# Gated cross-attention: another order of loads, stores and weight sums in the setup, and a later attention transpose

## The chip, the cores and the metric

The kernel runs on one core of a Trainium2 chip, in float32 throughout. The metric is device time in microseconds (us) from the first to the last instruction, as the median of repeated runs. The kernel before takes 1005.09 us (three runs, 1005.05 to 1005.89).

## The reference, cut to what matters

```python
def reference(hidden_states, memory, W_mem, W_gate, b_gate, norm_w):   # 8x1024x1024, 8x64x512
    memory_proj    = einsum('bme,de->bmd', memory, W_mem)              # mp
    scores         = einsum('bnd,bmd->bnm', hidden_states, memory_proj) / sqrt(D)
    attn           = softmax(scores, axis=-1)
    memory_context = einsum('bnm,bmd->bnd', attn, memory_proj)
    gate_input     = concatenate([hidden_states, memory_context], axis=-1)
    gate           = sigmoid(einsum('bnf,df->bnd', gate_input, W_gate) + b_gate)
    fused          = hidden_states + gate * memory_context
    return fused * rsqrt(mean(fused ** 2) + 1e-06) * norm_w
```

The gate's product splits in two: x times the first half of W_gate (W1 below), and the memory context times the second half (W2). Since the context is attn times mp, the second part is attn times (mp times W2), and mp times W2 plus the bias is a small matrix (512 x 1024) that is made once.

## The kernel before

**Setup.** The memory (512 rows for the whole batch) is multiplied by W_mem into eight banks of PSUM (`pm`), and VectorE copies these to the four tiles `mpT`, two column chunks each. From there three things happen.

- `mpT` itself is stored to DRAM as `mpd` (lines 233 to 235). Each batch later loads its part, `mpb`, for the scores.
- `mpT` is transposed back to rows by VectorE, into one large tile `mpq`, and stored as `mgd[0]` (lines 236 to 249). `mpq` lies in the pool `xqpool`, which has one buffer, and that buffer is also the staging tile `xq` for x. So x can't be loaded before the stores of `mpq` have landed.
- TensorE makes mp times W2 in eight pieces of 128 x 512, n = 0 to 7 (`pg`, lines 430 to 435). VectorE adds the bias of each into a staging tile `g`, and the tile is stored as `mgd[1]` (lines 436 to 438). The staging tiles are two buffers in turn, `mg` and `attnT`, so piece n waits until the store of piece n-2 has landed.

VectorE also works on W1 between these pieces. The main product is done as Strassen-Winograd in two levels: seven outer products (o = 1 to 7), each of seven inner ones (A to F, A twice). The sums of W1's blocks that this needs are the list `w1_tasks` (lines 262 to 270): four outer sums of 128 x 2048 and 28 inner ones of 128 x 512. They are handed out behind the pieces n = 0 to 4 in equal parts. Behind piece 5 come six transposes of x (the first part of the list `first`, line 422) and GpSimd's first sums (`inner_s`), behind piece 6 the rest of `first`. x is loaded behind piece 0 (`load_xq(0)`, line 440), and the norm's weight too.

**The main loop.** x is worked in 16 quads of 512 rows. A quad is 49 slots; a slot is one inner product, two by two matmuls of 128 x 128 by 128 x 256. The outer products run in the order o = 1, 6, 7, 5, 4, 2, 3. Work of other engines is hung on slots by hand: `at(slot, fn)` puts it in the program ahead of that slot's matmuls, in the order in which it was hung, and `keep_in_program_order` holds each engine's instructions in program order. `plan(q)` (line 472) hangs a quad's own work; the end of an outer product hangs the norm's work into the next quad (lines 729 to 745). Around the change, counted from a quad's first slot:

- 7: scores (`psT` on TensorE, copied to `sT`), and two sums of x for the outer products; 9: the scores are transposed (`sc`); 10: softmax, first half (maximum and difference on VectorE, exponential on ScalarE); 13: second half (sum, reciprocal, and the product that makes `e` the attention).
- 17: `transpose_attn`: TensorE transposes `e` into `pa`, ScalarE copies it into `attnT` with four copies.
- 20: `attn_difference`: VectorE takes one difference within `attnT`.
- 17 and 18: `square`, ScalarE's sums of squares of the quad before; with the second goes a square root. 9 to 14, 23 and 29: `norm` on VectorE.
- 25: the first use of `attnT` on TensorE (`pc`).

All loads and stores but the residual's go through the queue of SyncE (`load`, line 95), which issues in program order.

Of the kernel before, what the change touches and what calls it, by code (L numbers as in the profile page):

```python
# [15 lines left out]
P = 128  # L16
# [4 lines left out]
def tile_gated_cross_attention_rmsnorm(  # L21
# [43 lines left out]
    QT = 4 * P  # L65
    QPB = N // QT
    NQ = B * QPB
    BM = B * M
    KD = D // P
    KE = E // P  # L70
    H = 512
    C = 256
    NPAIR = BM // P
    SCALE = 1.0 / float(D) ** 0.5
    Q4 = D // 4
# [3 lines left out]
    xqpool = ctx.enter_context(tc.tile_pool(name="xqpool", bufs=1))  # L79
    apool = ctx.enter_context(tc.tile_pool(name="apool", bufs=1))  # L80
    rot = ctx.enter_context(tc.tile_pool(name="rot", bufs=2))
    small = ctx.enter_context(tc.tile_pool(name="small", bufs=1))
# [6 lines left out]
    def mm(o, lhsT, rhs, start, stop):  # L89
        pin(nc.tensor.matmul(o, lhsT, rhs, start=start, stop=stop, skip_group_check=True))  # L90

    def tt(eng, o, a, b, op):
        pin(eng.tensor_tensor(o, a, b, op))  # L93

    def load(o, i):
        pin(nc.sync.dma_start(o, i))

    def t4k(pool, shape, tag, name):
        return pool.tile(shape, F32, tag=tag, name=name)
# [7 lines left out]
    def bank(n, shape, name):  # L107
        return ps.tile(shape, F32, tag=banks[n % 5], name=name)
# [36 lines left out]
    for h in range(2):  # L145
        for i in range(4):
            load(w1[h][32 * i : 32 * (i + 1), :, :], w1r[i][:, 4 * h : 4 * h + 4, :])
    R11, R21, R12, R22, T4, T1, T2 = range(7)
    outer_b = {
        o: w1[h][:, :, c * H : (c + 1) * H]  # L150
# [6 lines left out]
    def w_op(o, s):  # L157
        if s >= T4:
            return inner_t[o][:, s - T4, :, :]
        k, n = {R11: (0, 0), R21: (1, 0), R12: (0, 1), R22: (1, 1)}[s]  # L160
        return outer_b[o][:, 2 * k : 2 * k + 2, n * C : (n + 1) * C]

    nw_sb = const.tile([P, D], F32, name="nw_sb")
# [7 lines left out]
    mpd = dram.tile([P, KD, BM], F32, name="mpd")  # L171
    mgd = dram.tile([2, BM, D], F32, name="mgd")
# [14 lines left out]
    def order_wm(k):  # L187
# [18 lines left out]
    mpT = [  # L206
        t4k(rot, [P, 2, BM], tag, f"mpT_{tag}_{i}")
        for tag in ("l2", "u")
        for i in range(2)
    ]  # L210

    def mp_rows(j, q):
        return mpT[j // 2][:, j % 2, q * P : (q + 1) * P]


    mpq = t4k(xqpool, [P, 4 * 4, Q4], "xq", "mpq")
    pm = [bank(j, [P, BM], f"pm{j}") for j in range(5)]
    pm += [ps_ctx.tile([P, BM], F32, tag="ctx", name=f"pm{j}") for j in (5, 6)]
    pm += [ps.tile([P, BM], F32, tag="sc", name="pm7")]
# [10 lines left out]
                )  # L230
    for j in range(KD):
        pin(nc.vector.tensor_copy(mpT[j // 2][:, j % 2, :], pm[j]))
    for j in range(0, KD, 2):
        src = mpT[j // 2]
        load(mpd[:, j : j + 2, :], src)
        for g in range(2):
            pin(
                nc.vector.transpose(
                    mpq.rearrange("p s (j r) -> p s j r", r=32)[
                        :, 8 * g : 8 * g + 8, j : j + 2, :  # L240
                    ],
                    src[:, :, g * C : (g + 1) * C].rearrange("p j (s c) -> p s j c", c=32),
                )
            )
    for i in range(4):
        load(
            mgd[0, :, i * Q4 : (i + 1) * Q4].rearrange("(s c) e -> c s e", c=32),
            mpq[32 * i : 32 * (i + 1), :, :],
        )


    def outer_sum(o, a, b):
        tt(nc.vector, outer_b[o], outer_b[a], outer_b[b], ALU.subtract)

    def inner_sums(o):
        for s, a, b in ((T1, R12, R11), (T2, R22, T1), (R12, R22, R12), (T4, R21, T2)):
            yield lambda s=s, a=a, b=b: tt(
                nc.vector, w_op(o, s), w_op(o, a), w_op(o, b), ALU.subtract
            )
# [6 lines left out]
        lambda: outer_sum(7, 3, 7),  # L266
        *(f for o in (7, 5) for f in inner_sums(o)),
        lambda: outer_sum(4, 2, 6),
        *(f for o in (6, 4, 2, 3) for f in inner_sums(o)),
    ]  # L270


    xq, A, S, L2, O = {}, {}, {}, {}, {}
    sTs, attns, attnTs, scs, mps, mgs = {}, {}, {}, {}, {}, {}
    KH = KD // 2

    def where(q, t=0):
        return q // QPB, (q % QPB) * QT + t * P

    def load_xq(q):  # L280
        b, n0 = where(q)
        xq[q] = t4k(xqpool, [P, 16, Q4], "xq", f"xq{q}")
        src = x[b, n0 : n0 + QT, :].rearrange("(s c) (i e) -> i c s e", c=32, i=4)
        for i in range(4):
            load(xq[q][32 * i : 32 * (i + 1), :, :], src[i])

    def transpose_x(q, t, half):

# [44 lines left out]
    def inner_s(q, o, part):  # L333
        l11, l12, l21, l22 = quarters(left(q, o))
        if part == 0:
            L2[q, o] = t4k(rot, [P, 4, 2, P], "l2", f"l2_{q}_{o}")
        s1, s2, s3, s4 = (L2[q, o][:, i, :, :] for i in range(4))
        if part == 0:
            tt(nc.gpsimd, s1, l21, l22, ALU.add)
            tt(nc.gpsimd, s2, s1, l11, ALU.subtract)  # L340
        else:
            tt(nc.gpsimd, s3, l11, l21, ALU.subtract)
            tt(nc.gpsimd, s4, l12, s2, ALU.subtract)
# [85 lines left out]
    done, n = 0, 0  # L429
    for h in range(2):  # L430
        cols = slice(h * H, (h + 1) * H)
        for q in range(NPAIR):
            pg = bank(n, [P, H], f"pg2_{h}_{q}")
            for k in range(KD):
                mm(pg, mp_rows(k, q), w2[k][:, cols], k == 0, k == KD - 1)
            stage = t4k(small, [P, H], ("mg", "attnT")[n % 2], f"g2_{h}_{q}")
            tt(nc.vector, stage, pg, bias_sb[:, cols], ALU.add)
            load(mgd[1, q * P : (q + 1) * P, cols], stage)
            if n == 0:
                load_xq(0)  # L440
                load(nw_sb, norm_w.partition_broadcast(P))
            if n < 5:
                while done < len(w1_tasks) * (n + 1) // 5:
                    w1_tasks[done]()
                    done += 1
            elif n == 5:
                for f in first[:6]:
                    f()
                for part in range(2):
                    inner_s(0, 1, part)  # L450
            elif n == 6:
                for f in first[6:]:
                    f()
            n += 1
# [7 lines left out]
    def at(slot, fn, *args):  # L462
        due.setdefault(slot, []).append(lambda: fn(*args))

    def mid(key, fn, *args):
        beside.setdefault(key, []).append(lambda: fn(*args))
# [5 lines left out]
    def plan(q):  # L472
        t0 = SLOTS * q
        nxt = q + 1 < NQ
        order = [o for o, _ in ORDER]
        for i, o in enumerate(order):
            for part, t in ((0, 1), (1, 5)):
                if i + 1 < len(order):
                    at(t0 + 7 * i + t, inner_s, q, order[i + 1], part)
                elif nxt:  # L480
                    at(t0 + 7 * i + t, inner_s, q + 1, order[0], part)
        at(t0 + 7, scores, q)
        at(t0 + 7, outer_s, q, 3)
        at(t0 + 7, outer_s, q, 4)
        at(t0 + 9, transpose_scores, q)
        at(t0 + 10, softmax_a, q)
        at(t0 + 13, softmax_b, q)
        at(t0 + 17, transpose_attn, q)
        at(t0 + 20, attn_difference, q)
        if not nxt:  # L490
            at(t0 + 5, load_last)
            return
        at(t0 + 2, load_xq, q + 1)
        for t in (2, 3):
            mid((q, 5), transpose_x, q + 1, t, 0)
            mid((q, 2), transpose_x, q + 1, t, 1)
        for i, t, half in ((36, 0, 0), (38, 1, 0), (43, 0, 1), (45, 1, 1)):
            at(t0 + i, transpose_x, q + 1, t, half)
        mid((q, 3), outer_s, q + 1, 1)
        mid((q, 3), outer_s, q + 1, 2)  # L500
        if (q + 1) % QPB == 0:
            at(t0 + 10, load_mp, (q + 1) // QPB)
            at(t0 + 49, load_mg, (q + 1) // QPB)

    slot = 0

    def step():
# [241 lines left out]
    for q in range(NQ):  # L749
        plan(q)  # L750
        for o, ext in ORDER:
            outer_product(q, o, ext)
# [29 lines left out]
```

## Time and profile before

| engine | busy, us | share of the span |
|---|---|---|
| TensorE (PE) | 975.3 | 97% |
| its weight loads (PEld) | 766.3 | 76% |
| VectorE (DVE) | 766.4 | 76% |
| GpSimd (POOL) | 687.3 | 68% |
| ScalarE (ACT) | 317.6 | 32% |

How to read it: the span is 1005.2 us. A busy TensorE is one that has a matmul under way, so the waits to look for are the places where that record has a gap. In a timeline, a row gives the start, the duration, the engine, the line, the operation, what is written from what, the shapes and the number of merged instructions; in brackets stands how long the engine sat idle before the row, and what ended that. Line 93 and line 96 are helpers, so rows are told apart by their tiles. The trace numbers no tiles: `it` and `t` are W1's inner and outer sums, `a` transposed x, `l` GpSimd's sums of it, `u` VectorE's running sums.

### The profile page before, as it was taken

The page shows a single profiled execution, that of the slowest core. Times are in us where ns is not written, and L with a number is a line of the kernel's source. Part 1 is how long each engine was busy: PE and PEld are TensorE (multiplying, and loading weights), DVE is VectorE, ACT ScalarE, POOL GpSimd, SP SyncE. Part 2 cuts the span into 40 slices and gives each one's busy share as a digit, 9 for nine tenths or more (in the row PEclk, how much of TensorE's full clock was granted, in tenths as well). Part 3 has the DMA queues.
Part 4 walks back from the last instruction along what each step waited for, and adds up shares of the span by engine and source line. Part 5 has one row for each costly group of instructions (what it writes and reads, how often), then busy time and mean ns, then how long its engine had stood idle before and what let it go on. Part 6 is the DMA issues. An engine that isn't in the chain of part 4 may idle for free.

```text
span 1005.2 us, 14277 instructions
## 1 busy us (share of the span) xinstructions
PE 975.3 (97%) x4944; PEld 766.3 (76%) x4944; DVE 766.4 (76%) x1486; ACT 317.6 (32%) x588; POOL 687.3 (68%) x851
## 2 busy tenths in 40 slices
PE   6998999999999999999999999999999999999995
PEld 4443788878878887888788788878888887888783
DVE  2556567878878787878788787878787887878777
ACT  0000113424331514333242415233333424152344
POOL 0001477878878687878788786878687887868772
PEclk9999899999999999999999999999999999999998
DMA  9995609273643828182735647291926465381612
GB/s 206 231 258 126 131 1 179 84 137 116 128 113 92 181 66 176 63 173 100 144 94 112 144 103 160 60 192 63 178 85 123 112 134 126 84 189 53 178 64 84
DMA packets 72056, 126.76 MB, mean 126 GB/s; under 512 B 12848, under 2 KB 49712, under 8 KB 71984
## 3 DMA queue, kind: packets, MB, share of 16 engines
q1 hardware_dynamic: 63344, 94.39, 37.3%
q0 software_dynamic: 8640, 31.46, 16.7%
q8 instruction: 39, 0.64, 0.3%
q14 instruction: 33, 0.27, 0.1%
HBM read 85.98 MB, written 39.85 MB: 125 GB/s over the span
## 4 chain that ended last, share of the span: by engine, by line
PE 83%; DVE 13%; issue 1%; DMA 1%; SPq 1%; ACT 0%; POOL 0%; DVEq 0%; ACTq 0%
PE kA L90 17%; PE pc L90 11%; PE kE L90 9%; PE kD L90 8%; PE kF L90 8%; PE kB L90 8%; PE kC L90 7%; PE psT L90 6%; PE pg L90 5%; DVE gate L547 4%; DVE gate L93 3%; PE pm L90 2%; DVE e L93 2%; DVE u L93 1%; DMA wm<-in_w_mem_t 1%
## 5 line engine op out<-in xcount | busy, mean ns | idle before, releaser
L93 POOL TENSOR_TENSOR gate<-gate,u 128x256 f32<-128x256 f32 x336 | 269.0, 831 | 122.4 <-DVE u L93 102.3
L93 POOL TENSOR_TENSOR l<-a 128x256 f32<-128x256 f32 x128 | 125.4, 980 | 162.1 <-DVE a L296 95.1
L518 ACT ACTIVATE gate<-gate 128x512 f32<-128x512 f32 x128 | 79.0, 629 | 397.4 <-DVE gate L93 397.4
L90 PE MATMUL pc<-mg,attnT 64*128 64x256 f32 x512 | 127.4, 389 | 0.0
L90 PE MATMUL kB<-it,l 128*128 128x256 f32 x448 | 116.0, 382 | 2.5 <-POOL l L93 2.5
L547 DVE SCALAR_TENSOR_TENSOR gate<-gate,ss,nw_sb 128x512 f32<-128x512 f32 x120 | 116.3, 979 | 1.1
L90 PE MATMUL kD<-it,l 128*128 128x256 f32 x448 | 115.9, 381 | 0.0
L90 PEld LDWEIGHTS pc<-mg,attnT 64*128 64x128 f32 x512 | 90.6, 186 | 29.7 <-issue 21.2
L90 PE MATMUL kA<-w,a 128*128 128x256 f32 x384 | 99.6, 382 | 1.7 <-DVE a L296 1.4
L90 PEld LDWEIGHTS kB<-it,l 128*128 128x128 f32 x448 | 85.5, 191 | 14.5 <-POOL l L93 2.9
L90 PEld LDWEIGHTS kD<-it,l 128*128 128x128 f32 x448 | 84.5, 191 | 11.0
L93 DVE TENSOR_TENSOR gate<-gate,pc 128x512 f32<-128x512 f32 x128 | 87.1, 681 | 5.8 <-ACT gate L518 5.8
L296 DVE STREAM_TRANSPOSE a<-xq 128x512 f32<-128x512 f32 x128 | 86.0, 693 | 0.0
L90 PEld LDWEIGHTS kA<-w,a 128*128 128x128 f32 x384 | 73.4, 192 | 13.0 <-DVE a L296 2.2
L93 POOL TENSOR_TENSOR l<-s 128x256 f32<-128x256 f32 x96 | 77.7, 809 | 8.1 <-PE kF L90 5.6
L93 DVE TENSOR_TENSOR u<-u,kB 128x256 f32<-128x256 f32 x112 | 46.8, 418 | 43.7 <-PE kB L90 39.7
L662 ACT COPY u<-kA 128x256 f32<-128x256 f32 x112 | 40.4, 361 | 92.2 <-PE kA L90 92.1
L90 PE MATMUL kE<-it,a 128*128 128x256 f32 x256 | 69.3, 393 | 0.0
L90 PE MATMUL kC<-w,l 128*128 128x256 f32 x256 | 66.7, 384 | 2.2 <-DVE g L93 2.2
L90 PE MATMUL kA<-t,s 128*128 128x256 f32 x256 | 67.4, 386 | 0.0
L93 DVE TENSOR_TENSOR gate<-gate,kE 128x256 f32<-128x256 f32 x112 | 45.3, 417 | 27.5 <-PE kE L90 22.6
L90 PE MATMUL kF<-w,l 128*128 128x256 f32 x256 | 65.7, 379 | 0.0
(102 smaller groups left out, 1961.4 us busy)
## 6 DMA issues: line engine op xcount, KB each, us to landing
xq<-in_x SPq DMA_DIRECT2D x64, 512.0 KB, 9.6
gate<-in_x POOLq DMA_DIRECT2D x60, 512.0 KB, 8.3
out<-gate SPq DMA_DIRECT2D x60, 512.0 KB, 2.6
w<-in_w_gate_t SPq DMA_DIRECT2D x32, 128.0 KB, 4.5
w<-in_w_gate_t SPq DMA_DIRECT2D x8, 512.0 KB, 14.5
mg<-mgd SPq DMA_DIRECT2D x16, 256.0 KB, 4.1
mgd<-mpq SPq DMA_DIRECT2D x4, 512.0 KB, 11.7
mgd<-g SPq DMA_DIRECT2D x8, 256.0 KB, 2.1
```

What stands on the lines that cost most here:

```text
L90: pin(nc.tensor.matmul(o, lhsT, rhs, start=start, stop=stop, skip_group_check=True))
L93: pin(eng.tensor_tensor(o, a, b, op))
L296: nc.vector.transpose(A[key][:, :, r * P : (r + 1) * P].rearrange("p j (s c) -> p s j c", c=32), xq[q].rearrange("p s (j r) -> p s j r", r ...
L518: pin(nc.scalar.activation(g, g, AF.Sigmoid))
L547: nc.vector.scalar_tensor_tensor(g[:, cols], g[:, cols], rstd[:, t % 2 : t % 2 + 1], nw_sb[:, cols], ALU.mult, ALU.mult,)
L662: pin(nc.scalar.copy(p1, kb["A"]))
```

## The change

Five edits go together.

1. mp's rows get four staging tiles of 128 x 1024 in the pool of transposed x (`a11` to `a22`) instead of one tile in x's own buffer. The eight transposes of 128 x 512 become sixteen of 128 x 256, and the four stores of 512 KB sixteen of 128 KB.
2. With x's buffer free, `load_xq(0)` and the load of `norm_w` move ahead of all stores. Behind them come the sixteen stores of `mgd[0]`, then the four of `mpd`, then the eight of the gate's pieces.
3. The gate's pieces have three staging tiles in turn: `mg`, `attnT`, `mpb`.
4. Eight of the 32 sums of W1 (the inner sums of o = 2 and 3) leave the setup for slots 2 to 5 and 10 to 13 of the first quad.
5. In every quad `transpose_attn` moves from slot 17 to 18 and `attn_difference` from 20 to 21.

The aim is to have x in early, to let VectorE wait less for stores in the setup, and to make room for the sums in the first quad.

```diff
+    xq = {}
+
+    def load_xq(q):
+        b, n0 = q // QPB, (q % QPB) * QT
+        xq[q] = t4k(xqpool, [P, 16, Q4], "xq", f"xq{q}")
+        src = x[b, n0 : n0 + QT, :].rearrange("(s c) (i e) -> i c s e", c=32, i=4)
+        for i in range(4):
+            load(xq[q][32 * i : 32 * (i + 1), :, :], src[i])
...
-    mpq = t4k(xqpool, [P, 4 * 4, Q4], "xq", "mpq")
+    mpq = [t4k(apool, [P, 4, Q4], f"a{i}{j}", f"mpq{i}{j}") for i in (1, 2) for j in (1, 2)]
...
-    for j in range(0, KD, 2):
-        src = mpT[j // 2]
-        load(mpd[:, j : j + 2, :], src)
-        for g in range(2):
+    load_xq(0)
+    load(nw_sb, norm_w.partition_broadcast(P))
+    for g in range(4):
+        for j in range(0, KD, 2):
             pin(
                 nc.vector.transpose(
-                    mpq.rearrange("p s (j r) -> p s j r", r=32)[
-                        :, 8 * g : 8 * g + 8, j : j + 2, :
-                    ],
-                    src[:, :, g * C : (g + 1) * C].rearrange("p j (s c) -> p s j c", c=32),
+                    mpq[g].rearrange("p s (j r) -> p s j r", r=32)[:, :, j : j + 2, :],
+                    mpT[j // 2][:, :, g * P : (g + 1) * P].rearrange(
+                        "p j (s c) -> p s j c", c=32
+                    ),
                 )
             )
-    for i in range(4):
-        load(
-            mgd[0, :, i * Q4 : (i + 1) * Q4].rearrange("(s c) e -> c s e", c=32),
-            mpq[32 * i : 32 * (i + 1), :, :],
-        )
+        for i in range(4):
+            load(
+                mgd[0, g * P : (g + 1) * P, i * Q4 : (i + 1) * Q4].rearrange(
+                    "(s c) e -> c s e", c=32
+                ),
+                mpq[g][32 * i : 32 * (i + 1), :, :],
+            )
+    for j in range(0, KD, 2):
+        load(mpd[:, j : j + 2, :], mpT[j // 2])
...
-        *(f for o in (6, 4, 2, 3) for f in inner_sums(o)),
+        *(f for o in (6, 4) for f in inner_sums(o)),
     ]
-
-
-    xq, A, S, L2, O = {}, {}, {}, {}, {}
+    w1_last = [f for o in (2, 3) for f in inner_sums(o)]
...
-            stage = t4k(small, [P, H], ("mg", "attnT")[n % 2], f"g2_{h}_{q}")
+            stage = t4k(small, [P, H], ("mg", "attnT", "mpb")[n % 3], f"g2_{h}_{q}")
             tt(nc.vector, stage, pg, bias_sb[:, cols], ALU.add)
             load(mgd[1, q * P : (q + 1) * P, cols], stage)
-            if n == 0:
-                load_xq(0)
-                load(nw_sb, norm_w.partition_broadcast(P))
...
-        at(t0 + 17, transpose_attn, q)
-        at(t0 + 20, attn_difference, q)
+        at(t0 + 18, transpose_attn, q)
+        at(t0 + 21, attn_difference, q)
...
+    for i, fn in enumerate(w1_last):
+        at((2, 3, 4, 5, 10, 11, 12, 13)[i], fn)
```

More of the change, by code (lines that the diff above doesn't have):

```diff
@@ L268, in tile_gated_cross_attention_rmsnorm @@
         lambda: outer_sum(4, 2, 6),
-        *(f for o in (6, 4, 2, 3) for f in inner_sums(o)),
+        *(f for o in (6, 4) for f in inner_sums(o)),
     ]
-    xq, A, S, L2, O = {}, {}, {}, {}, {}
+    w1_last = [f for o in (2, 3) for f in inner_sums(o)]
+    A, S, L2, O = {}, {}, {}, {}
     sTs, attns, attnTs, scs, mps, mgs = {}, {}, {}, {}, {}, {}
@@ L278, in where @@
         return q // QPB, (q % QPB) * QT + t * P
[L280 to L285, printed above, removed]
     def transpose_x(q, t, half):
```

## The prediction

> **What bounds the kernel now.** I read the page first: shares of the span, then the chain that ended last.
>
> ```profile
> PE 975.3 (97%) x4944; PEld 766.3 (76%) x4944; DVE 766.4 (76%) x1486; ACT 317.6 (32%) x588; POOL 687.3 (68%) x851
> PE 83%; DVE 13%; issue 1%; DMA 1%; SPq 1%; ACT 0%; POOL 0%; DVEq 0%; ACTq 0%
> ```
>
> TensorE is the bound. An edit that removes no matmul can win only where TensorE has a gap, so I read its timeline for gaps. There are two kinds. The first is at the seam between setup and main loop (TensorE, 36 to 190 us):
>
> ```profile
> 90.81 3.60 PE L90 MATMUL pg<-w,mpT_u 128*128 128x512 f32 x8
> 95.78 1.13 PE L90 MATMUL kA<-w,a 128*128 128x256 f32 x4 [1.38 <-DVE a L296]
> 99.42 2.04 PE L90 MATMUL kB<-it,l 128*128 128x256 f32 x4 [2.50 <-POOL l L93]
> 103.63 2.05 PE L90 MATMUL kC<-w,l 128*128 128x256 f32 x4 [2.17 <-DVE g L93]
> 110.98 3.67 PE L90 MATMUL psT<-a,mpb 128*64 128x256 f32 x32
> ```
>
> From the end of `pg` (94.4) to `psT` (110.98) pass 16.6 us for seven inner products, which take 0.86 each in later quads, 6.1 in all. Some 10.5 us are open here: gaps, and products at half pace behind them. VectorE holds the end: kC uses the PSUM bank of the gate's last piece `g`, which VectorE empties late. Why late, its own timeline says:
>
> ```profile
> 57.10 2.29 DVE L93 TENSOR_TENSOR t<-w,t 128x2048 f32<-128x2048 f32 x1 [5.30 <-DMA w<-in_w_gate_t]
> 70.64 0.69 DVE L93 TENSOR_TENSOR g<-pg,bias_sb 128x512 f32<-128x512 f32 x1 [5.19 <-DMA mgd<-g]
> 85.15 0.69 DVE L93 TENSOR_TENSOR g<-pg,bias_sb 128x512 f32<-128x512 f32 x1 [7.88 <-DMA mgd<-g]
> 95.03 3.66 DVE L296 STREAM_TRANSPOSE a<-xq 128x512 f32<-128x512 f32 x6
> 102.83 0.65 DVE L93 TENSOR_TENSOR g<-pg,bias_sb 128x512 f32<-128x512 f32 x1
> ```
>
> It waited 18.4 us: for W1, and twice for a staging tile whose store had not landed. After the last wait it works without a break from 85.15 to kC. SyncE's queue shows why stores land late:
>
> ```profile
> 50.69 7.98 SPq L96 DMA_DIRECT2D mgd<-mpq  x4
> 58.77 4.26 SPq L96 DMA_DIRECT2D mgd<-g  x1
> 69.92 2.12 SPq L96 DMA_DIRECT2D xq<-in_x  x4
> 72.73 31.11 SPq L96 DMA_DIRECT2D mgd<-g  x7
> ```
>
> x waits for `mpq`'s stores, and the second and third piece stand behind 2 MB of x.
>
> The second gap is in every quad but the first (TensorE in quad 0, then in quad 3, then from the waits of the whole run: total us, times, longest):
>
> ```profile
> 122.68 1.03 PE L90 MATMUL kC<-w,l 128*128 128x256 f32 x4
> 123.55 0.38 PE L392 MATMUL pa<-ident,e 128*128 128x128 f32 x2
> ```
>
> ```profile
> 288.57 1.03 PE L90 MATMUL kC<-w,l 128*128 128x256 f32 x4
> 289.81 0.41 PE L392 MATMUL pa<-ident,e 128*128 128x128 f32 x2 [0.20 <-DVE e L93]
> ```
>
> ```profile
> PE pa L392 <- DVE e L93: 3.1, 15, 0.2
> ```
>
> kC to `pa` takes 0.87 us in quad 0 and 1.24 in quad 3: 0.37 lost where VectorE has the norm's work and finishes `e` late. It fits the quads' lengths from `psT` to `psT`: 55.05 for the first (110.98 to 166.03), 55.45 later (276.87 to 332.32).
>
> **What the Trainium skill says.** (1) "SBUF — State Buffer", section on the DMA port swizzle: 32 partitions reach half of the ports, about 218 GB/s at most, 128 all, 436. The trace agrees: 226 GB/s from 37 to 57 us (W1, quarters of 32 partitions), 404 from 57 to 62 (mostly `mpd`, 128 partitions). So x and `mgd[0]`, both by quarters, stay slow in any order. (2) "TensorE: Matmul & The Clock Gate", section "What's actually happening": the array falls to half clock after an idle window and recovers after a busy one. Agrees: kB, 1.03 us later on, takes 2.04 here. (3) "SBUF — State Buffer", section "Who interferes with whom": a VectorE operation with two SBUF inputs and one of GpSimd exclude each other. Agrees: the GpSimd sum at 293.85 takes 0.91 instead of 0.73, beside `attn_difference` at 293.68.
>
> **The change part by part.**
>
> *Order of transfers.* Transfers on the queue landed in the order of issue, so I add their times up. W1 is in at 57.1 (the wait above), with nothing ahead of it changed. Behind it, in the new order: x, 11.3 (data from about 72, the last quarter issued at 71.73 landed 11.6 later, 83.3); `norm_w`, 1.0 (72.10 + 12.3 = 84.4); `mgd[0]`, 8.0 (from 61.9 to 58.13 + 11.8 = 69.9); `mpd`, 4.8 (57.1 to 46.85 + 15.0 = 61.9); the first piece, 0.6 (70.6 after 69.9). Sum 25.7, so the first piece lands at **82.8**. The sixteen small stores are new: W2's loads had their size and quarters and took 0.56 each (issued at 8.40 to 31.49, 32 of them, behind each other), 9.0 for sixteen; the page's best rate, about 404 GB/s, gives 5.2. I keep 8.0 and the ends for the range. The queue's own waits (on landings of earlier transfers) cost nothing: while one is held, the engines still have work queued.
>
> *Three staging tiles.* VectorE now stops at piece 3, not at pieces 2 and 3. It waits for the landing of piece 0's store, which now stands behind x and all of mp. So the wait ends at 82.8 + 0.1, against 85.15: **the third tile mostly turns two waits into one long one**, from about 67 on. x itself, in at 69.4 instead of 83.3, was not what ended last: its transposes start at 95.03 behind VectorE's sums.
>
> *An eighth of W1's sums, moved.* From piece 3 to the transposes VectorE takes 9.9 us before (85.15 to 95.03): three pieces and 13 inner sums of 0.61. After, tasks are dealt 4, 5, 5, 5, 5, so behind piece 3 lie ten, one of them the outer sum of 2.2 that ran in an earlier wait before: 9.9 - 4 x 0.61 + 2.2 = 9.7. **The eight sums (4.9 us) leave, but little of it leaves this stretch.** Transposes start at 82.9 + 9.7 = 92.6, 2.4 us sooner; from there to kC and `psT` the same work follows at the same pace. Gain **2.4 us**. In quad 0 the eight sums run on a VectorE that waits 1.9, 1.3 and 2.1 us for TensorE in slots 2 to 6 (free); in slots 10 to 13 four of them add 2.4 us, against 3.9 of norm work there in later quads. So quad 0's `e` comes some 1.5 to 2 us later, which the shifted transpose still hides.
>
> *Transposes by 256.* Sixteen at about 0.35 (half of 0.61, plus some fixed cost) are 5.6 instead of 4.9 us; they end before 46, as piece 0 is ready at 46.2. Nothing.
>
> *The attention transpose one slot later.* `e` is done at 289.65 in quad 3; slot 18 begins 0.86 later than slot 17, at 290.3 without the gap. The wait goes: 0.37 x 15 quads = 5.6. What may take its place: (a) ScalarE's copies now stand behind the second square and the square root with its table load (1.25 + 1.28 + 0.29, running from 289.3): they start near 292.1 instead of 290.25, end at 293.6, and the difference on VectorE, now behind the slot-20 sum, at 294.4, does not wait. (b) GpSimd's sum for slot 23's weights ended at 294.76, their load began at 295.02; with TensorE 0.37 earlier this would bind by up to 0.2, but the sum loses the difference beside it and should take 0.73. I take 0.35 a quad: **5.3 us**; ends 0.17 (2.6) and 0.38 (5.7).
>
> Sum: 1005.1 - 2.4 - 5.3 = **997.4**.
>
> **The rivals.**
>
> - *The setup gains nothing*: stores by quarters crawl at 180 GB/s (`mgd[0]` 11.5 us instead of 8.0), the first piece lands past 85. For it: those rates stood at the end of the old stores. Against: smaller stores change quarters sooner. 1005.1 - 5.3 = 999.8.
> - *Only the setup gains*: ScalarE or GpSimd takes over the 0.37. For: (b) is tight. 1002.7.
> - *The setup gains more*: stores of several quarters mix and run at 404 GB/s, 2.8 us sooner; 994.6. Beyond 5 us TensorE's own `pg`, to 94.4, holds the seam.
> - *Slower*: the copies behind square and root come late, `attn_difference` waits, all VectorE sums behind it slip, and TensorE loses 0.2 more a quad instead of winning (15 x 0.2 = 3.0), with the setup 1.0 worse: 1009.1. Against: 0.8 us of slack in (a).
>
> **How the numbers follow.** Forecast 0.60 (995.5 to 999); setup nothing 0.13; only setup 0.09; more 0.12; slower 0.06. The range 993.5 to 1001.5 leaves out the third, the last and a little of the fourth, some 0.18. Faster (below 1003.1): the first, second, fourth and half of the third, 0.90; same 0.04; slower 0.06.
>
> **What would show it.** One VectorE wait of about 15 us ending near 83 for the store of a gate piece; transposes at about 92.6, `psT` near 108.5; x landed near 69; no gap before `pa` in any quad, and 55.1 from `psT` to `psT`. Wrong if the piece's store lands much before 80 or after 86, or if a gap of 0.3 us turns up at slots 18 to 25 of each quad.

## The result, and the profile after

The changed kernel takes 995.92 us (994.48 to 997.58), the kernel before 1005.1 us: a ratio of 0.9909, 95% interval 0.9893 to 0.9924, that is 7.6 to 10.8 us less. Run a second time, beside other kernels, it gave 0.9897 (0.9882 to 0.9912).

The page of the changed kernel, shares of the span and the chain that ended last:

```profile
PE 967.9 (98%) x4944; PEld 765.2 (77%) x4944; DVE 770.7 (78%) x1494; ACT 319.4 (32%) x588; POOL 688.4 (69%) x851
PE 86%; DMA 5%; DVE 4%; SPq 2%; issue 1%; ACT 0%; POOL 0%; DVEq 0%; ACTq 0%
```

As many matmuls as before, 7.4 us less of TensorE's busy time, and a chain in which VectorE's 13% have become 4%. Of the 7.4 us, 4.1 lie at the seam (10.55 us busy between `pg` and `psT` before, 6.44 after), where in this profile nothing runs at half pace (half pace is an inner product in 2.04 us instead of 1.03). The seam, in TensorE's timeline:

```profile
90.51 3.60 PE L90 MATMUL pg<-w,mpT_u 128*128 128x512 f32 x8
93.94 1.03 PE L90 MATMUL kA<-w,a 128*128 128x256 f32 x4
94.86 1.10 PE L90 MATMUL kB<-it,l 128*128 128x256 f32 x4
99.10 1.10 PE L90 MATMUL kC<-w,l 128*128 128x256 f32 x4 [3.13 <-DVE g L93]
103.68 3.67 PE L90 MATMUL psT<-a,mpb 128*64 128x256 f32 x32
```

Of three gaps one is left, in front of kC; kC and what follows run at full pace; `psT` starts 7.3 us sooner (103.68 for 110.98). VectorE's timeline shows one wait for a store, and SyncE's queue the new order:

```profile
56.58 2.29 DVE L93 TENSOR_TENSOR t<-w,t 128x2048 f32<-128x2048 f32 x1 [2.35 <-DMA w<-in_w_gate_t]
80.81 0.69 DVE L93 TENSOR_TENSOR g<-pg,bias_sb 128x512 f32<-128x512 f32 x1 [14.55 <-DMA mgd<-g]
90.48 3.66 DVE L303 STREAM_TRANSPOSE a<-xq 128x512 f32<-128x512 f32 x6
98.30 0.65 DVE L93 TENSOR_TENSOR g<-pg,bias_sb 128x512 f32<-128x512 f32 x1
```

```profile
38.73 14.01 SPq L96 DMA_DIRECT2D xq<-in_x  x4
56.81 16.07 SPq L96 DMA_DIRECT2D mgd<-mpq  x16
76.39 22.91 SPq L96 DMA_DIRECT2D mgd<-g  x8
```

In the later quads the gap in front of `pa` is gone (TensorE in quad 3, then ScalarE, whose copies now follow the root without a pause):

```profile
281.65 1.03 PE L90 MATMUL kD<-it,l 128*128 128x256 f32 x4
282.51 0.38 PE L399 MATMUL pa<-ident,e 128*128 128x128 f32 x2
```

```profile
284.04 0.29 ACT L543 ACTIVATE ss<-ss,eps_sb 128x2 f32<-128x2 f32 x1
284.34 1.51 ACT L410 COPY attnT<-pa 64x256 f32<-64x256 f32 x4
```

`psT` to `psT` is 55.05 us in each of the fourteen later intervals (55.45 before, the first of them 55.39), but 55.31 in quad 0, which had 55.05. The two profiles differ by 12.5 us, more than the medians do: the run profiled before was 1.9 us above its median (1006.99 for 1005.1), the one after is the fastest of its six (994.48). The last experiment shows a part of the reason.

### The profile page after: what moved, and what is told of

Same layout as the page of the kernel before. It is cut to its first block, busy times and chain, and to the rows that moved or that the text cites. A ratio compares the mean times of both kernels' runs of the same rounds, so it can differ in the third digit from the quotient of the medians.

```text
span 992.7 us, 14303 instructions
## 1 busy us (share of the span) xinstructions
PE 967.9 (98%) x4944; PEld 765.2 (77%) x4944; DVE 770.7 (78%) x1494; ACT 319.4 (32%) x588; POOL 688.4 (69%) x851
## 4 chain that ended last, share of the span: by engine, by line
PE 86%; DMA 5%; DVE 4%; SPq 2%; issue 1%; ACT 0%; POOL 0%; DVEq 0%; ACTq 0%
PE kA L90 19%; PE pc L90 12%; PE kE L90 11%; PE kF L90 10%; PE kD L90 10%; PE kC L90 10%; PE kB L90 9%; PE psT L90 6%; DMA w<-in_w_gate_t 3%; SPq L96 2%; DVE gate L93 1%; DMA mgd<-mpq 1%; DVE a L303 0%; DMA mgd<-g 0%; DMA memq<-in_mem 0%
## 5 line engine op out<-in xcount | busy, mean ns | idle before, releaser
L553 DVE SCALAR_TENSOR_TENSOR gate<-gate,ss,nw_sb 128x512 f32<-128x512 f32 x120 | 124.7, 1048 | 1.1
L93 POOL TENSOR_TENSOR l<-s 128x256 f32<-128x256 f32 x96 | 75.4, 785 | 4.4 <-issue 2.5
```

The lines of the kernel that those rows point to most:

```text
L553: nc.vector.scalar_tensor_tensor(g[:, cols], g[:, cols], rstd[:, t % 2 : t % 2 + 1], nw_sb[:, cols], ALU.mult, ALU.mult,)
```

## Experiments

The theory (A): there are two separate gains. The later attention transpose takes a wait out of 15 quads; at the seam, what counts is when VectorE gets past its last wait for a gate piece's store, and how much work it still has behind that wait. Rivals are the other edits: the sums moved away, the loads in front, mp's rows apart.

**The attention transpose alone.** On the kernel before:

```diff
-        at(t0 + 17, transpose_attn, q)
-        at(t0 + 20, attn_difference, q)
+        at(t0 + 18, transpose_attn, q)
+        at(t0 + 21, attn_difference, q)
```

> The kernel before with edit 5 alone (attention transpose in slot 18, difference in slot 21). Theory A (the change has two separate gains: about 5.6 us from the wait in front of pa in 15 quads, the rest at the seam of setup and main loop): 1005.1 - 5.6 = 999.5 us, psT to psT 55.05 us in every quad, seam as before (pg to psT 16.6 us). Rival B (the later transpose only makes room for the sums in the first quad, and the quads got shorter because the work behind the seam starts sooner): no gain without the other edits, about 1005 us, 55.45 us a quad. Rival C (ScalarE's copies behind square and root cost part of it): 1001 to 1003 us, 55.2 to 55.3 a quad.

999.81 us, ratio 0.9941 (0.9924 to 0.9958), so 4.2 to 7.6 us. All quads take 55.05 us, and the seam is as it was (`psT` at 111.31). A holds, and B falls. C's price isn't there.

**The same edit undone in the changed kernel** (the lines above, the other way).

> The changed kernel with edit 5 undone (slots 17 and 20 again, all else as changed). Theory A: each of 15 quads takes back 0.40 us, and quad 0, where e is now finished at the time of slot 18, loses about 0.8 more: 995.9 + 6.0 + 0.8 = 1002.7 us. Rival B: the quads stay at 55.05 us, only quad 0 loses: 996.7 us.

1001.93 us, ratio 0.9964 (0.9951 to 0.9977) against 0.9909: some 5.5 to 6 us more than the changed kernel. Nearly all later quads are back at 55.45 us (one takes 55.13), and quad 0 takes 56.19. Its list of waits has the old one, longer at its longest, which is quad 0's:

```profile
PE pa L399 <- DVE e L93: 3.9, 15, 0.9
```

So the gain doesn't depend on the other edits, and the sums in slots 10 to 13 do need the later slot.

**The sums back in the setup.**

```diff
-        *(f for o in (6, 4) for f in inner_sums(o)),
+        *(f for o in (6, 4, 2, 3) for f in inner_sums(o)),
...
-    for i, fn in enumerate(w1_last):
-        at((2, 3, 4, 5, 10, 11, 12, 13)[i], fn)
```

> The changed kernel with edit 4 undone (all 32 sums of W1 in the setup, dealt over pieces 0 to 4 as before). Theory A (the moved sums left a stretch in which VectorE waited for a store anyway): from piece 3 to the transposes 9.9 instead of 9.7 us, quad 0 back from 55.31 to 55.05 us: 995.9 + 0.2 - 0.3 = 995.8 us, no change. Rival D (the eight sums are what made the seam shorter): VectorE reaches the transposes 4.9 us later, 1000.8 us or more.

996.8 us, ratio 0.9904 (0.9883 to 0.9925), against 0.9909 with the sums moved: no difference that can be seen. VectorE waits 9.3 us for piece 0's store instead of 14.6, and from there to the transposes it takes 9.9 us (79.19 to 89.07), as expected: the sums fill a wait. Quad 0 is back at 55.05 us. D falls.

```profile
79.19 0.69 DVE L93 TENSOR_TENSOR g<-pg,bias_sb 128x512 f32<-128x512 f32 x1 [9.30 <-DMA mgd<-g]
```

**Two staging tiles.**

```diff
-            stage = t4k(small, [P, H], ("mg", "attnT", "mpb")[n % 3], f"g2_{h}_{q}")
+            stage = t4k(small, [P, H], ("mg", "attnT")[n % 2], f"g2_{h}_{q}")
```

> The changed kernel with edit 3 undone (two staging tiles for the gate's pieces in turn). Theory A (the landing of piece 0's store at 80.7 us sets the seam): piece 2 now waits for it, and its five tasks and itself (3.7 us) come behind 80.8: transposes at 94.2 instead of 90.5, a longer gap of TensorE, and half pace behind it as in the kernel before: 3.7 to 6.5 us more, 999.6 to 1002.4 us. Rival E (the third tile only turns two waits into one, worth nothing): 995.9 us.

1000.9 us, ratio 0.995 (0.9934 to 0.9967): 5 us more than the changed kernel, and about what the attention transpose alone gives (0.9941). VectorE in this kernel:

```profile
81.44 0.69 DVE L93 TENSOR_TENSOR g<-pg,bias_sb 128x512 f32<-128x512 f32 x1 [18.15 <-DMA mgd<-g]
85.18 0.68 DVE L93 TENSOR_TENSOR g<-pg,bias_sb 128x512 f32<-128x512 f32 x1
90.51 0.68 DVE L93 TENSOR_TENSOR g<-pg,bias_sb 128x512 f32<-128x512 f32 x1
94.24 0.68 DVE L93 TENSOR_TENSOR g<-pg,bias_sb 128x512 f32<-128x512 f32 x1
94.84 3.66 DVE L303 STREAM_TRANSPOSE a<-xq 128x512 f32<-128x512 f32 x6
```

The wait ends about when it did (81.44 for 80.81), but four pieces (2 to 5) stand behind it instead of three, with their sums: 13.4 us to the transposes instead of 9.7. The seam is then as long as before the change (`psT` at 110.62), although loads, rows and sums are all as changed. E falls.

**Third tile and attention transpose alone**, on the kernel before: the edit of the first experiment, and

```diff
-            stage = t4k(small, [P, H], ("mg", "attnT")[n % 2], f"g2_{h}_{q}")
+            stage = t4k(small, [P, H], ("mg", "attnT", "mpb")[n % 3], f"g2_{h}_{q}")
```

> The kernel before with edits 3 and 5 alone (three staging tiles, attention transpose a slot later; mp's rows in x's buffer, stores in front of the loads, all sums of W1 in the setup, as before). Theory A (at the seam the third tile is what counts): piece 2 waits for nothing, piece 3 for the store of piece 0, which lands near 70.5, and the last wait is piece 4's, for the store of piece 1 behind x near 85; then two pieces and seven sums: transposes at about 90.7, as in the changed kernel (90.5): 996 us. Rival G (the third tile needs the separate rows and the loads in front): the seam stays as before, 999.8 us, as with edit 5 alone.

995.36 us, ratio 0.9901 (0.9882 to 0.9919), beside 0.9897 for the changed kernel on the same chip. Edit 5 and the one line of edit 3 give all of it. In the profile the last wait is piece 4's, at 82.62 (earlier than expected: all transfers ran some 3 us ahead of those in the kernel before's profile, piece 0's store landing at 67.5), with little behind it:

```profile
82.62 0.69 DVE L93 TENSOR_TENSOR g<-pg,bias_sb 128x512 f32<-128x512 f32 x1 [9.37 <-DMA mgd<-g]
88.16 3.67 DVE L296 STREAM_TRANSPOSE a<-xq 128x512 f32<-128x512 f32 x6
```

The profiled run is the fastest of its six (991.81 us, the others 993.16 to 998.67), so this timeline is not that of the median. What shows the effect of the tile is the time, beside the 999.81 us of the attention transpose alone (on another chip: ratios 0.9901 and 0.9941).

**mpd's stores behind piece 2**, in the changed kernel:

```diff
-    for j in range(0, KD, 2):
-        load(mpd[:, j : j + 2, :], mpT[j // 2])
...
             load(mgd[1, q * P : (q + 1) * P, cols], stage)
+            if n == 2:
+                for j in range(0, KD, 2):
+                    load(mpd[:, j : j + 2, :], mpT[j // 2])
```

> The changed kernel with the four stores of mpd put behind the store of piece 2 instead of in front of piece 0. Theory A (the landing of piece 0's store sets the seam): it lands 5.0 us sooner (80.7 - 5.0 = 75.7), transposes start at about 85.4, TensorE goes from pg to kC without the gap of 3.1 us (kC's bank is then free right behind pg): 995.9 - 3.1 = 992.8 us. Rival D (VectorE's amount of work sets the seam, not the store): no change, 995.9 us.

990.97 us, ratio 0.9855 (0.9835 to 0.9875). VectorE's wait for piece 0's store ends 3.2 us sooner than in the changed kernel's profile (77.59), not 5.0; W1 was in 1.5 us later in this run (58.06 for 56.58). The seam is closed all the same:

```profile
95.27 1.03 PE L90 MATMUL kB<-it,l 128*128 128x256 f32 x4
96.41 1.10 PE L90 MATMUL kC<-w,l 128*128 128x256 f32 x4
```

The gain, about 5 us, is more than the gap of 3.1. In this trace nothing at the seam runs at half pace; the changed kernel has half pace behind its gap in one of two profiles (last experiment). That this makes up the rest fits, but wasn't tested.

**x behind the stores**, in the changed kernel:

```diff
-    load_xq(0)
-    load(nw_sb, norm_w.partition_broadcast(P))
...
             load(mgd[1, q * P : (q + 1) * P, cols], stage)
+            if n == 0:
+                load_xq(0)
+                load(nw_sb, norm_w.partition_broadcast(P))
```

> The changed kernel with the loads of x and norm_w put back behind the store of piece 0 (mp's rows still in their own tiles). Theory A (x in front of the stores costs time, since piece 0's store lands behind 12 us of loads, while x is not needed before 90 us): piece 0 lands at about 69, piece 1 behind x near 81, VectorE waits for piece 1 at piece 4 instead: transposes at 81 + 0.6 + 3.1 + 0.6 = 85.5, no gap before kC, 995.9 - 3.1 = 992.8 us. Rival F (all loads in front of the stores is where the gain at the seam comes from): x lands at 80 and VectorE or TensorE waits for it, or the seam goes back to the length before: 995.9 + 2 to + 7 us.

991.85 us, ratio 0.9866 (0.9848 to 0.9883), 4 us less than with the loads in front. VectorE waits twice, and the second wait, for piece 1 behind x, has only pieces 4 and 5 behind it; of the gap before kC 0.39 us is left:

```profile
69.19 0.69 DVE L93 TENSOR_TENSOR g<-pg,bias_sb 128x512 f32<-128x512 f32 x1 [3.59 <-DMA mgd<-g]
82.94 0.69 DVE L93 TENSOR_TENSOR g<-pg,bias_sb 128x512 f32<-128x512 f32 x1 [8.34 <-DMA mgd<-g]
86.69 0.68 DVE L93 TENSOR_TENSOR g<-pg,bias_sb 128x512 f32<-128x512 f32 x1
```

Rival F falls: in front of all stores the loads cost time, since piece 0's store, which VectorE needs first, lands behind them, and x isn't needed before 90 us. They need not cost it: the experiment before this one leaves the loads in front, puts `mpd`'s stores late, and is as fast. And mp's rows apart may be worth something after all: this kernel (0.9866, 0.9848 to 0.9883) is some 3.5 us below the third tile and attention transpose alone (0.9901, 0.9882 to 0.9919), with intervals that barely touch. The two differ in the rows, in where `mpd`'s stores stand and in the moved sums; which of these counts wasn't tested.

**mpd's stores late and the sums back** (the edits of both experiments).

> The changed kernel with mpd's stores behind piece 2 and all 32 sums of W1 back in the setup. Theory A: the store of piece 0 lands at 75.7, transposes at 75.8 + 9.9 = 85.7, still soon enough for kC; quad 0 has no gap before pa and takes 55.05 us: 992.8 - 0.3 = 992.5 us. Rival D (the moved sums shorten the seam): 4.9 us later transposes and a gap before kC: 995 us or more.

991.26 us, ratio 0.9862 (0.9845 to 0.988): as with mpd's stores late alone. The 0.3 us of quad 0 is won (55.05), but a new wait is in front of the scores: TensorE waits 1.16 us for the load of `mpb`, and `psT` starts at 102.11.

**The load of mpb ahead of piece 7's store**, in that kernel:

```diff
             elif n == 6:
+                load_mp(0)
                 for f in first[6:]:
                     f()
...
-    load_mp(0)
     load_mg(0)
```

> The kernel with mpd's stores behind piece 2 and all sums of W1 in the setup, and the load of mpb put in front of piece 7's store. In that kernel without this, TensorE waited 1.16 us in front of psT for this load. Theory A: the wait goes, kernel time 991.3 - 1.1 = 990.1 us, psT directly behind kF, near 101. Rival H (the load lands late in any place, because mpd's stores land at 83 to 84 and piece 7's work holds the queue): 991.3 us.

991.0 us, ratio 0.9849 (0.9836 to 0.9861). The wait is gone (`psT` at 100.52, 0.96 behind kF's start). By time these four kernels (`mpd`'s stores late, x behind the stores, and the last two) can't be told apart; each is some 4 to 5 us faster than the changed kernel. This one has no gap of TensorE over 0.15 us between 20 us and the last quad.

**The stores of mp's rows by quarter.**

```diff
-        for i in range(4):
+    for i in range(4):
+        for g in range(4):
             load(
```

> The changed kernel with the sixteen stores of mgd[0] in the order of quarters (four stores of one quarter of 32 partitions, then the next quarter) instead of rotating quarters. If rotating quarters is what made these stores faster than before (6.6 instead of 8.0 us from norm_w's landing to the last of them), they take about 8 us again, piece 0's store lands 1.4 us later, and the seam grows by 1.4 us: 997.3 us. If the size of the stores or the loads in front made them faster: 6.6 us, 995.9 us.

998.86 us, ratio 0.9932 (0.9918 to 0.9947). From `norm_w`'s landing to the last of the sixteen stores pass 8.0 us (68.35 to 76.31) instead of 6.6 (68.34 to 74.94), and VectorE's wait ends 1.2 us later (82.05 for 80.81).

So the order of the quarters made these stores faster, not their size: the same sixteen transfers of 128 KB, in the order of the old ones, take the old 8.0 us. The changed kernel's second profile has the speed of the first (247 and 248 GB/s over 4 us in which only these stores were under way; 193 in the order of quarters). The time grew by 2.9 us, more than the 1.4; a part of that is open. In this profile kC and a part of kD ran at half pace, which those of the changed kernel's first profile did not, but those of its second did.

**The changed kernel again.**

> The changed kernel itself, once more, beside the other two on one chip. If the half pace of TensorE behind the gap before kC depends on where the gap falls in time and not on its length (3.13 us of gap without half pace here so far, 2.36 us with it in the kernel with the sums put back), a second profile can show the same gap of about 3 us with or without it, psT at 103.7 or at about 105.5 to 106.5; the median stays at 996 us. If the length of the gap decides, psT is at 103.7 again.

995.99 us. TensorE has a gap of the same length in front of kC (and one of 0.34 us in front of kB, which the first profile lacks), but this time half pace behind it:

```profile
99.54 2.04 PE L90 MATMUL kC<-w,l 128*128 128x256 f32 x4 [3.13 <-DVE g L93]
101.38 1.64 PE L90 MATMUL kD<-it,l 128*128 128x256 f32 x4
105.54 3.67 PE L90 MATMUL psT<-a,mpb 128*64 128x256 f32 x32
```

kC to `psT` takes 6.0 us here, 4.6 in the first profile, 7.35 in the kernel before. The same program gets one or the other, so the length of the last gap alone doesn't decide. That fits what the Trainium skill, "TensorE: Matmul & The Clock Gate", section "What's actually happening", says of a window that runs on its own and isn't started by the kernel. No trace here shows the window itself, and the page's length for it, about 3.4 us, is more than any single gap behind which half pace was seen: 3.13 us here, 2.36 with the sums back in the setup, 2.50 before the change. All profiles of this case with two or more gaps of over 0.3 us at the seam have half pace there. Of those with one such gap the kernel with the sums back (2.36) has it, and the first profile (3.13), the transpose undone (2.74), the third tile with the attention transpose (1.41) and x behind the stores (0.39) don't.

The granted clock at the seam was 0.69 before the change (94.4 to 111 us), 1.00 in the first profile after it and 0.85 in this one; the means of the whole runs are 0.996 and 0.994. The ten runs of the changed kernel have means of 0.993 to 0.996, and only two of them 0.996; the sixteen runs of the four kernels with `mpd`'s stores or x moved back, which have at most 0.39 us of gap before kC, all have 0.996 or 0.997. So half pace behind the gap looks more usual than its absence. That is read from means, not from traces.

## Why the prediction was right, and where it was not

**Right in time and in the larger part.** 997.4 was forecast, 995.9 measured, inside the range. The attention transpose was to give 5.3 us with ends of 2.6 and 5.7; alone it gave 5.9 (4.2 to 7.6), and the quads' length fell by 0.40 to 55.05, the 55.1 that was named. That is a little more than the 0.37 of the gap: `pa` itself took 0.41 us behind the gap and takes 0.38 without. Both points that might have taken its place behaved as argued. (a) The copies end at 285.85, and the difference at 286.59 doesn't wait. (b) GpSimd's first sum behind the difference's old place now takes 0.73 us.

**The seam was mis-sized, and credited to the wrong edit.** Forecast were 2.4 us, with `psT` at 108.5; the profiles have 103.68 and 105.54, and the medians of its two measurements leave 3 to 4.5 us beside the attention transpose. That the total lay inside the range owes something to luck: the range was wide enough for a seam whose gain came from another edit than the one that was named. Three terms:

- *Order of transfers*: piece 0's store was to land at 82.8 and landed at 80.7 (issued at 76.39, 4.3 later). The term that was off most is `mgd[0]`, 6.6 us instead of 8.0; I had kept the old time because the rotating quarters were untried. The statement behind it, that transfers by quarters stay slow in any order, holds for x but not for these stores: while they alone were under way, the DMA engines moved 248 GB/s (70 to 74 us), and 193 in the order of quarters (71 to 75 us). The first is above the 218 that the prediction took from the Trainium skill as the most for 32 partitions, and W1's 226 was above it too, so "agrees" was too much. W1 and x were half a microsecond better each; `mpd` took 5.1 instead of 4.8.
- *Half pace*: "from there to kC and `psT` the same work follows at the same pace" is the step that failed. Transposes came 4.55 us sooner (90.48), and from there to kC the work took 8.6 us as before. From kC to `psT` TensorE took 1.4 us less than before in one profile and 2.8 in the other, since half pace was short or absent. Why it was is argued from the fewer gaps, not shown.
- *Three staging tiles*: "the third tile mostly turns two waits into one long one" was put down without a gain, and the gain was booked on the order of transfers. The runs show the reverse. Without the third tile the new order leaves the seam as it was (`psT` at 110.62 for 110.98); with the third tile and the old order it is as good as the whole change (995.36). The tile shifts the last wait by a piece, so that a piece and its sums come out from behind it. Loads ahead of all stores cost 4 us of what was to be had.

**The moved sums** gain nothing, as reckoned: VectorE took 9.67 us from piece 3 to the transposes, against 9.7, and undoing that edit changes nothing measurable. The claim that the shifted transpose still hides them in quad 0 was a little off (55.31 instead of 55.05). A sum was to take 0.6 us; here are two of them, and the wait behind:

```profile
113.83 1.24 DVE L93 TENSOR_TENSOR w<-w 128x512 f32<-128x512 f32 x1
...
115.32 0.88 DVE L93 TENSOR_TENSOR it<-w,it 128x512 f32<-128x512 f32 x1
```

```profile
116.24 1.03 PE L90 MATMUL kD<-it,l 128*128 128x256 f32 x4
117.34 0.41 PE L399 MATMUL pa<-ident,e 128*128 128x128 f32 x2
```

They took up to 1.24 us while GpSimd was adding, so `e` was ready at 117.2 and slot 18 at 117.1. The exclusion cited in the prediction for GpSimd works on VectorE too; I had used it on one side only.

Left open: the profiled spans differ by 12.5 us, the medians by 9 to 10. Half pace explains up to 2.8 us of such differences, and it was in the profile of before and not in the first of after; how often it comes was seen only through the mean clocks above.

## What to carry to other kernels

When an engine works in order and waits for a buffer, don't only ask when the wait ends: count the work that stands behind it in the program. One more buffer that moves the last wait behind a piece of work can be worth more than a faster transfer, and work that only fills a wait is free, so taking it away wins nothing. Put in front of the store that is waited for only what is needed before it.

## What was not expected of the hardware

Sixteen stores of 128 KB from 32 partitions each took 6.6 us when neighbours in the queue lay on different quarters of the partitions, and 8.0 when four in a row lay on the same. The same program had a gap of 3.13 us in front of kC with TensorE at full pace behind it in one run and at half pace for 3.3 us in another.
